# Layer 3 of a four-layer graph network: the new state turned by VectorE and transfers instead of TensorE

## The chip, the cores and the metric

The kernel runs on one core of one Trainium2 chip. The metric is the device time of a run in microseconds (us). The engines of a core, each with its own instruction queue that is worked off in order, are TensorE (matmuls; the profile calls it PE, and its loads of the stationary operand PEld), VectorE (DVE), ScalarE (ACT), GpSimd (POOL) and SyncE (SP), which here only issues transfers. SBUF is the working memory of 128 partitions, PSUM takes what TensorE writes, in 8 banks of 128 x 512 floats, and device memory holds inputs and outputs.

## The reference

128 graphs of 64 nodes with 256 features go through four layers, each of the form `x = layernorm(x + layer(x, adj))`, all in float32. Layers 0 to 2 are graph convolutions and are not touched here. Layer 3 is a gated graph network, five rounds with one set of gate weights:

```
A = (adj != 0)
h = x
for l in range(5):
    m   = h @ weight[l]
    agg = A^T @ m                      # for each graph
    gi, gh = agg @ w_ih.T + b_ih, h @ w_hh.T + b_hh
    r = sigmoid(gi_r + gh_r);  z = sigmoid(gi_z + gh_z)
    n = tanh(gi_n + r * gh_n)
    h = (1 - z) * n + z * h
out = layernorm(x + h * mask)
```

So each round needs the state `h` in two layouts. The gate products contract over features and take `h` with features in the partitions. The aggregation over neighbours contracts over nodes and takes `h` with nodes in the partitions. The gates produce the new state with features in the partitions.

## The kernel before

Two graphs make a pair of 128 nodes, and eight graphs (four pairs) make a chunk, so there are 16 chunks. A chunk's state with nodes in the partitions is a tile of 128 x 4 pairs x 256 features (`xt`, and from the second round on `h`); with features in the partitions it is 128 x 2 halves x 512 nodes (`hT`, and when new `hn`). `weight[l]` and `w_ih` are folded into one matrix `V[l]`, so that the aggregation works on `h` itself: `messages` calls `gather`, whose matmuls have the state as stationary operand (loaded into the array) and the 0/1 adjacency `A01` as moving operand, and ScalarE copies the result to `agg`.

The gate products are done by a scheme of seven products for a 2 x 2 block matrix: GpSimd forms sums of the operand (`sums`, tiles `Th` of the state and `Ta` of `agg`), and `rz(i)` (reset and update gate, four products each) and `n(i)` (candidate, two products each) are the seven products, i from 1 to 7, in an order that fits the accumulation in PSUM. VectorE and ScalarE bring the parts together. `n(7)`, `n(4)` and `n(3)` end the round: `reset` forms the candidate's argument, `update` does the tanh and the new state, first for the feature half j=1 (in `n(4)`), then for j=0 (in `n(3)`).

The loop over s (lines 985 to 1031) runs through 80 steps of one chunk and one round each; two chunks alternate. Step s does the products of chunk x and, laid in between, the rest of the work of the chunk w of the step before: `w.n(4)` and `w.n(3)` after the first products of x, then `w.turn(1)` and `w.turn(0)`, four TensorE transposes each, through PSUM and a ScalarE copy into `h` (in the last round VectorE adds it to `xt` from PSUM), and at last `w.close()`, which gathers for w's next round. `filler` lays in the work of layers 1 and 2 for the two chunks to come (`mid`), in pieces.

TensorE's instruction order is the program's own, as written. On the other engines a scheduler orders the instructions when the program is built; `high_priority` brings one forward. Tiles of one name share a fixed number of buffers (`bufs`), and a tile waits until the buffer's readers are done. PSUM banks of the gate products come from a pool of five (`pg`), all others of layer 3 from one of three (`pt`).

The lines that matter: L208 the gather's matmuls, L212 its copies, L757 the gate products, L774 copies of partial products, L798 transposes on TensorE, L941 the copy into `h`, L946 the last round's add, L737 to L739 the sums on GpSimd, L853 to L862 reset and update, L964 the stores of the output, L189 and L197 the loads of adjacency and of `x` for the chunks to come.

Of the kernel before, what the change touches and what calls it, by code (L numbers as in the profile page):

```python
# [9 lines left out]
F32 = mybir.dt.float32  # L10
AF = mybir.ActivationFunctionType
ALU = mybir.AluOpType
# [3 lines left out]
B, N, D, HID, L = 128, 64, 256, 512, 5  # L16
# [10 lines left out]
NCH = B // CB  # L27
NP = CB // 2
# [40 lines left out]
def gnn_stack(  # L69
# [33 lines left out]
    dram = ctx.enter_context(tc.tile_pool(name="dram", bufs=1, space=bass.MemoryType.DRAM))  # L103
# [10 lines left out]
    powers, evictions, relus, tanhs = [], [], [], []  # L114
# [52 lines left out]
    ov = out.rearrange("(c p two) n d -> c (two n) p d", p=NP, two=2)  # L167
# [24 lines left out]
    def load_x(c):  # L192
# [6 lines left out]
                )  # L199
        xts[c] = xt  # L200

    def gather(src, m, name, pool=keep, tag="ag", bufs=1):

        a = pool.tile([128, 2, NP * 128], F32, tag=tag, name=name, bufs=bufs)
        for k in range(2):
            p = psum("pa")
            for q in range(NP):
                nc.tensor.matmul(  # L208
                    p[:, q * 128 : (q + 1) * 128], src[:, q, k * 128 : (k + 1) * 128], m[:, q, :], start=True, stop=True
                )  # L210
            with tc.high_priority():
                nc.scalar.copy(a[:, k, :], p)  # L212
        return a
# [4 lines left out]
    def mid(c):  # L218
# [28 lines left out]
        poly = keep.tile([128, NP, 128], F32, tag="poly", name="poly3", bufs=2)  # L247
# [6 lines left out]
        AT1 = keep.tile([128, NP, 128], F32, name="AT1", bufs=1)  # L254
        p = psum("pT1").rearrange("p (q n) -> p q n", q=NP)
# [9 lines left out]
        xt = xts.pop(c)  # L265
        p = psum("pp").rearrange("p (q n) -> p q n", q=NP)
        for q in range(NP):
            nc.tensor.matmul(p[:, q, :], An[:, q, :], poly[:, q, :], start=True, stop=True)
        poly = keep.tile([128, NP, 128], F32, tag="poly", name="poly1", bufs=2)
        with tc.high_priority():  # L270
            nc.vector.scalar_tensor_tensor(poly, dg, cw[:, 1:2], p, op0=ALU.mult, op1=ALU.add)
        ag = gather(xt, AT1, "ag1")
        nc.vector.tensor_add(xt, xt, l1bs[:, None, :].to_broadcast([128, NP, D]))
        p = psum("pp").rearrange("p (q n) -> p q n", q=NP)
        for q in range(NP):
            nc.tensor.matmul(p[:, q, :], An[:, q, :], poly[:, q, :], start=True, stop=True)  # L276
        poly = keep.tile([128, NP, 128], F32, tag="poly", name="poly0", bufs=2)
# [19 lines left out]
        yield  # L297


        ag = gather(xt, poly, "ag2")  # L300
        yield
        for u in range(NP // 2):
            p = psum("pd").rearrange("p (q d) -> p q d", q=2)
# [484 lines left out]
    class Chunk:  # L788
# [11 lines left out]

        def state_of_layer2(self, k):
            if k:
                self.hT = work.tile([128, 2, NP * 128], F32, tag="hT", name="hT", bufs=4)
            p = self.transpose(lambda q, k: self.xt[:, q, k * 128 : (k + 1) * 128], k, "pT3")
            nc.scalar.copy(self.hT[:, k, :], p)
            if not k:
                self.th = sums(self.hT, "h")

        def messages(self, h=None):
            self.agg = gather(self.xt if h is None else h, self.A01, "agg", work, "agg", 2)  # L810
            self.ta = sums(self.agg, "a")

        def rz(self, i):
# [19 lines left out]
        def n(self, i):  # L833
            if i == 1:
                self.NI = keep.tile([128, 2, 2, NP * 128], F32, tag="NI", name="NI", bufs=2)
                self.gn = Gates(
                    self.NI, [[(V[self.l], 2, self.agg, self.ta)], [(WHH, 2, self.hT, self.th)]], "n"
                )
            self.gn.product(i)
            I, n, r = self.NI[:, 0], self.NI[:, 1], self.RZ[:, 0]  # L840
            if i == 7:
                self.reset(1, slice(H, 2 * H), I[:, 1, H:], n[:, 1, H:])
            elif i == 4:
                self.reset(1, slice(0, H), self.gn.a[:, 0, :], self.gn.a[:, 1, :])
                self.hn = work.tile([128, 2, NP * 128], F32, tag="hT", name="hn", bufs=4)
                self.update(1)
            elif i == 3:
                self.reset(0, slice(0, 2 * H), I[:, 0, :], n[:, 0, :])
                self.update(0)

        def reset(self, j, f, i, h):
            n, r = self.NI[:, 1], self.RZ[:, 0]
# [75 lines left out]

        def turn(self, k):

            last = self.l == L - 1
            if k:
                self.hT = self.hn
                if not last:
                    self.h = work.tile([128, NP, D], F32, name="h", bufs=1)
            p = self.transpose(lambda q, k: self.hT[:, k, q * 128 : (q + 1) * 128], k, "pT4")
            pv = p.rearrange("p (q f) -> p q f", q=NP)
            f = slice(k * 128, (k + 1) * 128)
            if not last:
                with tc.high_priority():  # L940
                    nc.scalar.copy(self.h[:, :, f], pv)  # L941
                if not k:
                    self.th = sums(self.hT, "h")
            else:
                for q in range(NP):
                    nc.vector.scalar_tensor_tensor(  # L946
                        self.xt[:, q, f], pv[:, q, :], mask[:, self.c * NP + q : self.c * NP + q + 1], self.xt[:, q, f],
                        op0=ALU.mult, op1=ALU.add,
                    )

        def close(self, norm=None):
            if self.l < L - 1:
                self.messages(self.h)
            else:
                if norm:
                    mv, rs, _ = norm
                    nb = small.tile([128, NP], F32, name="nb")
                    nc.vector.scalar_tensor_tensor(nb, mv[:, :, 0], -1.0, rs, op0=ALU.mult, op1=ALU.mult)
                    with tc.issue_after(tanhs[-1].ins):
                        norm_apply(self.xt, mv, rs, nb, "a")  # L960
                else:
                    layernorm(self.xt, "a")
                for h in range(2):
                    nc.sync.dma_start(ov[self.c][:, 2 * h : 2 * h + 2], self.xt[:, 2 * h : 2 * h + 2])  # L964
            self.l += 1

# [18 lines left out]
    for s in range(NCH * L):  # L985
        u, t = s // (2 * L) * 2, s % (2 * L)
        if t == 0:
            for _ in filler:
                pass
            if u + 2 < NCH:  # L990
                for c in (u + 2, u + 3):
                    load_adj(c)
                    load_x(c)
                filler = both(mid(u + 2), mid(u + 3))
        if s == NCH * L - 1:
            break
        x, w = rows[s % 2], before
        nxt = None
        x.rz(1)
        if w:  # L1000
            w.n(4)
        x.rz(2)
        if w:
            w.n(3)
        x.rz(6)
        next(filler, None)
        x.rz(5)
        x.rz(7)
        x.n(1)
        if w:  # L1010
            w.turn(1)
            if w.l == L - 1 and w.c + 2 < NCH:
                nxt = Chunk(w.c + 2)
                nxt.state_of_layer2(1)
        x.rz(4)
        if w:
            w.turn(0)
            if nxt:
                nxt.state_of_layer2(0)
        x.n(6)  # L1020
        x.rz(3)
        if w:
            w.close()
            if nxt:
                nxt.messages()
                rows[(s + 1) % 2] = nxt
        x.n(2)
        x.n(5)
        next(filler, None)
        x.n(7)  # L1030
        before = x

    x, w = rows[1], before
# [4 lines left out]
    w.n(4)  # L1038
    x.rz(2)
    w.n(3)  # L1040
    x.hn = work.tile([128, 2, NP * 128], F32, tag="hT", name="hn", bufs=4)
    x.NI = keep.tile([128, 2, 2, NP * 128], F32, tag="NI", name="NI", bufs=2)
    for i in (6, 5, 7):
        x.rz(i)
# [74 lines left out]
```

## Time and profile before

| | |
|---|---|
| median of 3 runs (lowest to highest) | 2191.71 us (2191.57 to 2192.38) |
| span of the profiled execution | 2190.0 us |
| instructions in it | 30124 |
| VectorE busy | 1357.1 us |
| ScalarE busy | 1003.3 us |
| GpSimd busy | 573.1 us |
| moved by transfers | 51.12 MB |

The profiled execution has only its span; it lies 1.7 us below the median of the runs. A group in the profile is read as: line, engine, operation, tile written <- tiles read, shapes, xcount | busy us, mean ns of one | us that the engine sat idle before it, and what ended that. An fp32 matmul counts as two instructions there, a transpose as one. The busy time of an engine is the time in which at least one instruction of its own was under way; TensorE's instructions overlap one another, so the step from one start to the next says more than a duration. The chain that ended last is followed back from the last instruction, at each step to what released it.

### The profile page before, as it was taken

The page shows a single profiled execution, that of the slowest core. Times are in us where ns is not written, and L with a number is a line of the kernel's source. Part 1 is how long each engine was busy: PE and PEld are TensorE (multiplying, and loading weights), DVE is VectorE, ACT ScalarE, POOL GpSimd, SP SyncE. Part 2 cuts the span into 40 slices and gives each one's busy share as a digit, 9 for nine tenths or more (in the row PEclk, how much of TensorE's full clock was granted, in tenths as well). Part 3 has the DMA queues.
Part 4 walks back from the last instruction along what each step waited for, and adds up shares of the span by engine and source line. Part 5 has one row for each costly group of instructions (what it writes and reads, how often), then busy time and mean ns, then how long its engine had stood idle before and what let it go on. Part 6 is the DMA issues. An engine that isn't in the chain of part 4 may idle for free.

```text
span 2190.0 us, 30124 instructions
## 1 busy us (share of the span) xinstructions
PE 2175.2 (99%) x11538; PEld 1908.2 (87%) x11538; DVE 1357.1 (62%) x3033; ACT 1003.3 (46%) x1846; POOL 573.1 (26%) x622
## 2 busy tenths in 40 slices
PE   9999999999999999999999999999999999999998
PEld 6777888898988889888889898889898898888887
DVE  3345666566766676666766666657656666566556
ACT  3333334544544554444444454445444544455454
POOL 3211131232332222222322232232222222232222
PEclk9999999999999999999999999999999999999999
DMA  6532110000100010000000010001000000000000
GB/s 166 180 120 67 48 38 3 1 3 1 42 1 3 1 39 4 3 1 20 22 3 1 1 42 1 3 1 42 1 1 1 20 10 1 1 10 11 1 1 20
DMA packets 54236, 51.12 MB, mean 23 GB/s; under 512 B 20942, under 2 KB 49100, under 8 KB 54092
## 3 DMA queue, kind: packets, MB, share of 16 engines
q1 hardware_dynamic: 49412, 43.95, 6.6%
q0 software_dynamic: 1968, 4.83, 0.8%
q8 instruction: 91, 1.49, 0.3%
q10 hardware_dynamic: 2712, 0.42, 0.1%
q14 instruction: 53, 0.43, 0.1%
HBM read 32.40 MB, written 16.78 MB: 22 GB/s over the span
## 4 chain that ended last, share of the span: by engine, by line
PE 97%; DVE 2%; POOL 0%; issue 0%; DMA 0%; ACT 0%; SPq 0%; POOLq 0%; DVEq 0%; ACTq 0%
PE parz L757 25%; PE pan L757 12%; PE pdrz L757 12%; PE pa L208 9%; PE pbrz L757 6%; PE pdn L757 6%; PE ps L458 4%; PE ph L442 4%; PE pT L798 4%; PE pbn L757 3%; PE pd L286 3%; PE pd L307 3%; PE pa L426 1%; PE po L480 1%; PE pf L578 1%; PE pp L276 1%
## 5 line engine op out<-in xcount | busy, mean ns | idle before, releaser
L774 ACT COPY c<-parz 128x512 f32<-128x512 f32 x240 | 140.6, 586 | 320.4 <-PE parz L757 319.8
L757 PE MATMUL parz<-Th,WHH 128*128 128x256 f32 x960 | 285.9, 379 | 0.2 <-ACT c L774 0.2
L757 PE MATMUL parz<-Ta,V 128*128 128x256 f32 x960 | 285.8, 379 | 0.0
L737 POOL TENSOR_TENSOR Th<-hn 128x512 f32<-128x512 f32 x64 | 81.4, 1272 | 725.2 <-DVE hn L862 602.8
L774 ACT COPY c<-pan 128x512 f32<-128x512 f32 x237 | 138.9, 586 | 149.7 <-PE pan L757 149.7
L859 ACT ACTIVATE NI<-NI,bih 128x512 f32<-128x512 f32 x158 | 113.9, 721 | 201.6 <-DVE NI L854 201.5
L757 PEld LDWEIGHTS parz<-Ta,V 128*128 128x128 f32 x960 | 182.5, 190 | 24.7
L757 PEld LDWEIGHTS parz<-Th,WHH 128*128 128x128 f32 x960 | 176.3, 190 | 21.2 <-ACT c L774 0.7
L831 ACT ACTIVATE RZ<-RZ,brz 128x512 f32<-128x512 f32 x158 | 114.7, 726 | 136.6 <-DVE RZ L786 136.6
L786 DVE TENSOR_TENSOR RZ<-pdrz,c 128x512 f32<-128x512 f32 x80 | 55.0, 688 | 191.7 <-PE pdrz L757 191.7
L737 POOL TENSOR_TENSOR Ta<-agg 128x512 f32<-128x512 f32 x80 | 101.9, 1274 | 266.1 <-ACT agg L212 266.1
L137 POOL TENSOR_TENSOR rs<-ve,mhalf 128x4 f32<-128x4 f32 (+2 forms) x65 | 67.2, 1035 | 286.1 <-DVE ve L135 222.9
L757 PE MATMUL pan<-Ta,V 128*128 128x256 f32 x474 | 141.3, 380 | 0.0
L757 PE MATMUL pan<-Th,WHH 128*128 128x256 f32 x474 | 141.1, 379 | 0.0
L780 DVE TENSOR_TENSOR NI<-pbn,c 128x512 f32<-128x512 f32 x79 | 54.6, 692 | 127.4 <-PE pbn L757 110.2
L208 PEld LDWEIGHTS pa<-A,h 128*128 128x128 f32 x1024 | 124.4, 192 | 3.3
L208 PE MATMUL pa<-A,h 128*128 128x128 f32 x1024 | 124.6, 275 | 0.0
L776 DVE TENSOR_TENSOR NI<-pdn,c 128x512 f32<-128x512 f32 x79 | 54.4, 689 | 113.0 <-ACT c L774 113.0
L860 DVE TENSOR_TENSOR RZ<-hn,NI 128x512 f32<-128x512 f32 x126 | 86.5, 686 | 48.5 <-ACT NI L859 48.5
L862 DVE TENSOR_TENSOR hn<-RZ,NI 128x512 f32<-128x512 f32 x158 | 108.4, 686 | 1.8
L861 DVE TENSOR_TENSOR RZ<-RZ 128x512 f32<-128x512 f32 x158 | 108.2, 685 | 1.8
L458 PE MATMUL ps<-W,hg 128*125 128x256 f32 (+5 forms) x464 | 103.6, 380 | 0.3 <-ACT v L313 0.3
(228 smaller groups left out, 5056.1 us busy)
## 6 DMA issues: line engine op xcount, KB each, us to landing
out_dram<-xt SPq DMA_DIRECT2D x30, 256.0 KB
W<-in_w_dram SPq DMA_DIRECT2D x10, 512.0 KB
xt<-xb SPq DMA_DIRECT2D x32, 156.0 KB
xo<-in_x_dram SPq DMA_DIRECT2D x9, 512.0 KB
xb<-xo SPq DMA_DIRECT2D x9, 512.0 KB
xt<-xa SPq DMA_DIRECT2D x32, 100.0 KB
xg<-in_x_dram SPq DMA_DIRECT2D x25, 125.0 KB
xa<-xg SPq DMA_DIRECT2D x25, 125.0 KB
```

What stands on the lines that cost most here:

```text
L208: nc.tensor.matmul(p[:, q * 128 : (q + 1) * 128], src[:, q, k * 128 : (k + 1) * 128], m[:, q, :], start=True, stop=True)
L442: nc.tensor.matmul(p, W1[:, u.g, k, e * 128 : (e + 1) * 128], ag0[:, k, : u.cols], start=k == 0, stop=k == 1)
L458: nc.tensor.matmul(p[: u.rows[t], t - v, :], hg[:, e, u.off[t] : u.off[t] + u.rows[t]], W2[:, u.g, e, :], start=e == 0, stop=e == 3,)
L737: nc.gpsimd.tensor_sub(t[:, 0:2, :], a[:, :, H:], a[:, 0, :].rearrange("p (s n) -> p s n", s=2))
L757: nc.tensor.matmul(bank[:, g, :], w[:, q, i - 1, :], rhs, start=i in (1, 2, 5) and g == 0 and m == 0, stop=m == len(side) - 1, skip_group_ ...
L774: nc.scalar.copy(c, self.a)
L798: nc.tensor.transpose(p[:, q * 128 : (q + 1) * 128], src(q, k), ident)
L831: nc.scalar.activation(RZ[:, q, 0, :], RZ[:, q, 0, :], AF.Sigmoid, bias=b[0])
L859: nc.scalar.activation(n, n, AF.Tanh, bias=bih[:, 4 + j : 5 + j])
L860: e.tensor_sub(d, self.hT[:, j, f], n)
L861: e.tensor_mul(d, d, z)
L862: e.tensor_add(self.hn[:, j, f], d, n)
```

## The change

A chunk's new state is no longer transposed by TensorE. A new function `flip` follows each `update`: VectorE transposes the state half in blocks of 32 x 32 into a tile `flip`, in which the four pairs lie innermost; SyncE stores that to a buffer `hb` in device memory; and after the second half four transfers, one for each 32 partitions, bring both halves back as `h`, now 128 x 256 features x 4 pairs. The gather of rounds 1 to 4 takes its stationary operand from there, a column of features with a step of four floats. In the last round VectorE adds from `h` to `xt` in `close`. Only for chunk 14's last round does `turn` remain.

`w.n(4)` and `w.n(3)` move out of the following step into their own, to its end; `n(2)` comes earlier; `w.close()` with the gather now comes after `x.n(7)`, ahead of `x.n(4)` and `x.n(3)`. The state's sums for GpSimd follow directly on the update. `hT` and `hn` have three buffers instead of four.

```diff
         def messages(self):
+            src = halves(self.xt)
+            if self.l:
+                h = self.h
+                src = lambda q, k: h[:, k * 128 : (k + 1) * 128, q]
+            self.agg = gather(src, self.A01, "agg", work, "agg", 2)
...
             elif i == 4:
...
-                self.hn = work.tile([128, 2, NP * 128], F32, tag="hT", name="hn", bufs=4)
+                self.hn = work.tile([128, 2, NP * 128], F32, tag="hT", name="hn", bufs=3)
                 self.update(1)
+                self.flip(1)
             elif i == 3:
                 self.reset(0, slice(0, 2 * H), I[:, 0, :], n[:, 0, :])
                 self.update(0)
+                self.flip(0)
+                if self.l < L - 1:
+                    self.hT = self.hn
+                    self.th = sums(self.hT, "h")
+
+        def flip(self, j):
+
+            if self.c == NCH - 2 and self.l == L - 1:
+                return
+            if j:
+                self.hb = dram.tile([2, 128, NP * 128], F32, name="hb", bufs=2)
+            with tc.high_priority():
+                t = work.tile([128, NP, 32, NP], F32, name="flip", bufs=2)
+                nc.vector.transpose(
+                    t.rearrange("p r f q -> p q r f"), self.hn[:, j, :].rearrange("p (q r f) -> p q r f", q=NP, r=NP)
+                )
+                nc.sync.dma_start(self.hb[j], t.rearrange("p r f q -> p (r f q)"))
+                if not j:
+                    self.h = work.tile([128, D, NP], F32, name="h", bufs=1)
+                    hv = self.hb.rearrange("j (a i) (r c) -> r i (j a) c", i=32, r=NP)
+                    for r in range(NP):
+                        nc.sync.dma_start(
+                            self.h[32 * r : 32 * (r + 1)].rearrange("p (a f) q -> p a (f q)", f=32), hv[r]
+                        )
...
         x, w = rows[s % 2], before
         nxt = None
-        x.rz(1)
-        if w:
-            w.n(4)
-        x.rz(2)
-        if w:
-            w.n(3)
-        x.rz(6)
+        for i in (1, 2, 6):
+            x.rz(i)
         next(filler, None)
         x.rz(5)
         x.rz(7)
         x.n(1)
-        if w:
-            w.turn(1)
-            if w.l == L - 1 and w.c + 2 < NCH:
-                nxt = Chunk(w.c + 2)
-                nxt.state_of_layer2(1)
+        x.n(2)
+        if w and w.l == L - 1 and w.c + 2 < NCH:
+            nxt = Chunk(w.c + 2)
+            nxt.state_of_layer2(1)
         x.rz(4)
-        if w:
-            w.turn(0)
-            if nxt:
-                nxt.state_of_layer2(0)
+        if nxt:
+            nxt.state_of_layer2(0)
         x.n(6)
         x.rz(3)
+        x.n(5)
+        next(filler, None)
+        x.n(7)
         if w:
             w.close()
             if nxt:
                 nxt.messages()
                 rows[(s + 1) % 2] = nxt
-        x.n(2)
-        x.n(5)
-        next(filler, None)
-        x.n(7)
+        x.n(4)
+        x.n(3)
         before = x
...
         def close(self, norm=None):
+            self.l += 1
+            if self.l < L:
+                self.messages()
+                return
...
+                for q in range(NP):
+                    m = self.c * NP + q
+                    y = self.xt[:, q, :]
+                    nc.vector.scalar_tensor_tensor(
+                        y, self.h[:, :, q], mask[:, m : m + 1], y, op0=ALU.mult, op1=ALU.add
+                    )
+                layernorm(self.xt, "a")
```

More of the change, by code (lines that the diff above doesn't have):

```diff
@@ L200, in load_x, with halves @@
         xts[c] = xt
+    def halves(x):
+        return lambda q, k: x[:, q, k * 128 : (k + 1) * 128]
     def gather(src, m, name, pool=keep, tag="ag", bufs=1):
@@ L207, in gather @@
             for q in range(NP):
-                nc.tensor.matmul(
-                    p[:, q * 128 : (q + 1) * 128], src[:, q, k * 128 : (k + 1) * 128], m[:, q, :], start=True, stop=True
-                )
+                nc.tensor.matmul(p[:, q * 128 : (q + 1) * 128], src(q, k), m[:, q, :], start=True, stop=True)
             with tc.high_priority():
@@ L271, in mid @@
             nc.vector.scalar_tensor_tensor(poly, dg, cw[:, 1:2], p, op0=ALU.mult, op1=ALU.add)
-        ag = gather(xt, AT1, "ag1")
+        ag = gather(halves(xt), AT1, "ag1")
         nc.vector.tensor_add(xt, xt, l1bs[:, None, :].to_broadcast([128, NP, D]))
@@ L297, in mid @@
         yield
-        ag = gather(xt, poly, "ag2")
+        ag = gather(halves(xt), poly, "ag2")
         yield
@@ L802, in state_of_layer2 @@
             if k:
-                self.hT = work.tile([128, 2, NP * 128], F32, tag="hT", name="hT", bufs=4)
+                self.hT = work.tile([128, 2, NP * 128], F32, tag="hT", name="hT", bufs=3)
             p = self.transpose(lambda q, k: self.xt[:, q, k * 128 : (k + 1) * 128], k, "pT3")
@@ L807, in state_of_layer2, with messages @@
                 self.th = sums(self.hT, "h")
-        def messages(self, h=None):
-            self.agg = gather(self.xt if h is None else h, self.A01, "agg", work, "agg", 2)
+        def messages(self):
+            src = halves(self.xt)
[3 more added lines that the diff above has]
+            self.agg = gather(src, self.A01, "agg", work, "agg", 2)
             self.ta = sums(self.agg, "a")
@@ L929, in turn @@
         def turn(self, k):
[L931 to L936, printed above, removed]
+            p = self.transpose(lambda q, k: self.hn[:, k, q * 128 : (q + 1) * 128], k, "pT4")
             pv = p.rearrange("p (q f) -> p q f", q=NP)
             f = slice(k * 128, (k + 1) * 128)
[L939 to L943, printed above, removed]
+            for q in range(NP):
+                m = self.c * NP + q
+                nc.vector.scalar_tensor_tensor(
+                    self.xt[:, q, f], pv[:, q, :], mask[:, m : m + 1], self.xt[:, q, f], op0=ALU.mult, op1=ALU.add
+                )
@@ L944, in turn, with close @@
+        def close(self, norm=None):
+            self.l += 1
+            if self.l < L:
+                self.messages()
+                return
+            if norm:
+                mv, rs, _ = norm
+                nb = small.tile([128, NP], F32, name="nb")
+                nc.vector.scalar_tensor_tensor(nb, mv[:, :, 0], -1.0, rs, op0=ALU.mult, op1=ALU.mult)
+                with tc.issue_after(tanhs[-1].ins):
+                    norm_apply(self.xt, mv, rs, nb, "a")
             else:
                 for q in range(NP):
+                    m = self.c * NP + q
+                    y = self.xt[:, q, :]
@@ L946, in turn @@
                     nc.vector.scalar_tensor_tensor(
-                        self.xt[:, q, f], pv[:, q, :], mask[:, self.c * NP + q : self.c * NP + q + 1], self.xt[:, q, f],
-                        op0=ALU.mult, op1=ALU.add,
-                    )
[L951 to L965, printed above, removed]
+                        y, self.h[:, :, q], mask[:, m : m + 1], y, op0=ALU.mult, op1=ALU.add
+                    )
@@ L970, in gnn_stack @@
+                layernorm(self.xt, "a")
+            for h in range(2):
+                nc.sync.dma_start(ov[self.c][:, 2 * h : 2 * h + 2], self.xt[:, 2 * h : 2 * h + 2])
     rows = []
@@ L1037, in gnn_stack @@
     x.rz(1)
-    w.n(4)
     x.rz(2)
-    w.n(3)
-    x.hn = work.tile([128, 2, NP * 128], F32, tag="hT", name="hn", bufs=4)
+    x.hn = work.tile([128, 2, NP * 128], F32, tag="hT", name="hn", bufs=3)
     x.NI = keep.tile([128, 2, 2, NP * 128], F32, tag="NI", name="NI", bufs=2)
```

## The prediction

> **What bounds the kernel now.** I read the engines' busy times, then the chain that ended last, whole and piece by piece in one stretch of layer 3.
>
> ```profile
> PE 2175.2 (99%) x11538; PEld 1908.2 (87%) x11538; DVE 1357.1 (62%) x3033; ACT 1003.3 (46%) x1846; POOL 573.1 (26%) x622
> PE 97%; DVE 2%; POOL 0%; issue 0%; DMA 0%; ACT 0%; SPq 0%; POOLq 0%; DVEq 0%; ACTq 0%
> ```
>
> TensorE is never without work, and 97% of the chain is its own. So the change is worth what it takes out of TensorE's row, less what it makes slower in that row and less any hole that it opens. A matmul's shown duration overlaps the next one's, so prices come from the chain in order of time (start, length, name, count):
>
> ```profile
> 644.12 0.86 PE pan L757 x4
> 644.99 0.44 PE pT L798 x4
> 645.42 1.73 PE parz L757 x8
> 647.15 0.44 PE pT L798 x4
> 647.59 0.86 PE pan L757 x4
> 648.46 1.73 PE pdrz L757 x8
> 650.18 1.78 PE pa L208 x16
> 651.97 0.87 PE pbn L757 x4
> ```
>
> An fp32 product appears as two passes: 0.216 us a pass of 256 columns, so 0.431 a product; the gather `pa` takes 1.78/16 = 0.111 us a pass of 128 columns; a turn `pT` takes 0.109. A step of one chunk and one layer is 42 products (18.1), 8 gather products (1.78) and 8 turns (0.87), 20.8 us in all.
>
> ```profile
> L208 PE MATMUL pa<-A,h 128*128 128x128 f32 x1024 | 124.6, 275 | 0.0
> L208 PEld LDWEIGHTS pa<-A,h 128*128 128x128 f32 x1024 | 124.4, 192 | 3.3
> L798 PE MATMUL pT<-ident,hn 128*128 128x128 f32 x632 | 94.8, 273 | 0.0
> L798 PEld LDWEIGHTS pT<-ident,hn 128*128 128x128 f32 x632 | 79.0, 141 | 15.9
> L941 ACT COPY h<-pT 128x512 f32<-128x512 f32 x128 | 75.3, 588 | 0.0
> ```
>
> The reader sees 632 turns of the state, and that every gather pass has its own load of 128 weights: there the load row is as busy as the matmul row. In the gather the state `h` is the loaded operand.
>
> **What the Trainium skill says.** "TensorE: Matmul & The Clock Gate", LDWEIGHTS: columns divided by 1.2 in ns, so 107 for 128; the gather's 111 ns a pass agrees, and says that it stands at the load's own rate. "Advanced Engine Details and Errata", Memory Cachelines: SBUF has lines of 16 bytes, and it takes at least two hits on a line to absorb the access latency; another line at every access is penalised. For VectorE the trace shows this, in layer 0's sums:
>
> ```profile
> L502 DVE TENSOR_TENSOR F<-F,z 128x384 f32<-128x384 f32 x4 | 2.2, 549 | 0.0
> L502 DVE TENSOR_TENSOR F<-F,z 128x126 f32<-128x126 f32 x8 | 2.0, 288 | 4.6 <-ACT z L484 4.6
> L502 DVE TENSOR_TENSOR F<-F,z 128x64 f32<-128x64 f32 x4 | 1.1, 271 | 3.9 <-ACT z L484 3.9
> L502 DVE TENSOR_TENSOR F<-F,z 128x6 f32<-128x6 f32 x8 | 0.9, 159 | 0.0
> ```
>
> `F` has 15 floats a graph. The 384 and 126 elements are in runs of six and three, and with the 6 they lie on one line: 1.03 ns an element. On it the 64 should take 219 ns; they are in runs of one, 60 bytes apart, and took 271: 52/64 = 0.81 ns more an element, 1.8 times the rate. "VectorE: DVE Perf Modes", The three transpose paths: blocks of 32x32 only, 311 ns for 128x128 in bf16; no run here shows one. "DMA: Bandwidth & Descriptors", Latency and other measured facts: some 2 us of fixed cost; the queue of SyncE agrees:
>
> ```profile
> 1027.78 1.36 SPq L964 DMA_DIRECT2D out_dram<-xt  x2
> 1030.95 0.28 SPq L197 DMA_DIRECT2D xt<-xa  x1
> ```
>
> The load waits for the second store of 256 KB, issued at 1028.75: it landed after 2.2 us.
>
> **The change, part by part.**
>
> Turns. Of 632, the 8 of the chunk before the last remain. 624 x 0.109 = 68 us off the row that sets the end. Their 128 copies (75.3 us of ScalarE) and the last layer's adds from PSUM cost and give nothing directly: ScalarE is 46% busy and no step of the chain.
>
> Gather. `h` becomes 256 features by 4 pairs, so the 128 weights of a pass lie 16 bytes apart, each on a line of its own; before they were adjacent. Layers 1 to 4 of 16 chunks do it: 64 gathers, 1024 passes. The trace has no such load, so I bound it. Below: nothing (the load may not be limited by the line); a gain has no reason. Above: VectorE's 0.81 ns, or half the rate, gives 128 x 0.81 = 104 ns or 107 ns more a pass; and if what is fixed is VectorE's 1.85 ns a line, 237 ns a pass, 126 more. I take half the rate: 1.66 us a gather, and 64 of them 106 us (129 at most). The loads cannot hide, since the matmul beside each needs only 0.107. The whole turns at 68/1024 = 66 ns a pass: above it the change loses, below it wins.
>
> Transposes. 156 on VectorE, read in order, written 16 bytes apart. Four of the skill's price is 1.24 us, an ordinary 128x512 takes 0.69, and 512 x 0.81 on top of that gives 1.1: I take 1.1, ends 0.7 and 1.6. That is 172 us (109 to 250) onto VectorE's 62%. The cover is TensorE's step; uncovered, it counts only through the lateness of `h`.
>
> Transfers. 156 stores of 256 KB and 312 loads of 128 KB on SyncE's queue, 82 MB more than the 51 now, or some 45 GB/s over layer 3; the early slices show 180. Bandwidth is no matter, latency is. Take the end of `n(3)` as 0. `n(4)` ended at -0.9. VectorE then has the two resets of `n(4)` (0.9), an add (0.6), the long reset (1.3) with the tanh under it, both updates (3.6), one 0.6 of the next chunk, and the two transposes (2.2), at the back-to-back spacing of its rows (0.6 for a shown 0.69): last transpose done near 8.7. Store 2.2 to 3.0 (3.0 is the slowest seen in layer 0's stores). Four issues of 0.4 put the last load 1.2 later, and it lands 2.0 to 3.1 after that: `h` is there at 14.3 to 16.2. The gather now stands behind 38 products, at 16.4. So it is covered with 0.2 to 2.1 us to spare; steps with work of layers 0 to 2 laid in give TensorE up to 7 us more, but the step that holds the adjacency's preparation adds some 6 us to VectorE and only 0.4 to TensorE. I count 0.5 us in 14 such steps: 7 us, ends 0 and 40. The only buffer of `h` is free: the gather that read it ended some 15 us before. Two waits now have the state's transfers queued behind them on SyncE: a store of the output that waits for ScalarE's norm, with loads of `xt` that wait for that store's landing (2.2 us, as above), and a load of adjacency that waits for a VectorE read. Who waits in the end is the gather. At 2.2 us in each of 14 chunks that is 31 us, inside the ends. In the last layer VectorE itself waits for `h` (56 adds of 128x256), with the add for `n(7)` and the resets queued behind it, whose reader is the next chunk's bank 5 us later: if `h` is in time as above, nothing.
>
> Order. `n(4)` and `n(3)` move into their own step, behind the gather. Behind it come `n(4)` and `n(3)` (4 products), `rz(1)` and `rz(2)` of the other chunk (8) and one of `rz(6)` before GpSimd's sums `Ta` are needed: 13 products, 5.6 us. In the trace it is 3.0 us from the gather's end (1003.59) to the end of L738 on GpSimd (1006.56). The evicted `agg` is needed 5 products (2.1 us) after the gather; an eviction takes 0.58. A PSUM bank is asked for again at the soonest some 2 us after its reader (`rz(4)`'s sigmoids, then `n(5)`). `hT` with 3 buffers holds the three states alive at a time. All at nothing: the products named are the cover, and without it each us late is a us of hole per step, 80 in all.
>
> Sum against the span of 2190.0: -68 + 106 + 7 = 2235; the median of the runs stands 1.7 above the span, so 2236.7, say 2236.
>
> **Rivals.**
>
> *Loads at full rate.* If TensorE's port has line rate to spare, the gather stays at 0.111. For it: the skill's TensorE page puts weights at 1.2 a ns but columns at 2.4, and no TensorE row here shows a penalty. Against: 0.81 ns in the L502 row. Then 2190 - 68 + 7 + 1.7 = 2131. This one ends on the other side, from 66 ns a pass down.
>
> *The state comes late.* If transposes take 1.6 (+1.0), or loads in 512-byte pieces land in 5 us instead of 3, `h` is 2 us past the gather in nearly every step: 64 x 2 = 128 us of holes, as waits of `pa` for a transfer. 2357 with the slow loads, 2259 without. Against: the sum above leaves time even at the long ends of both transfers.
>
> *No difference.* A partial penalty near 66 ns with the holes at nothing: 2188 to 2196. Only coincidence speaks for it.
>
> **How the numbers follow.** Half rate, `h` in time: 0.49, own range 2208 to 2265 (a price of 85 to 129 us, holes of 0 to 40). Full rate, in time: 0.31, 2122 to 2170. A penalty of some 20 to 50 ns a pass: 0.04, 2145 to 2180. Late state: 0.13. Nothing: 0.03. The predicted time is the first case's, 2236. From 2124 to 2265 the range holds most of the first two and a little of the third: 8 in 10. A measurement tells 0.2%, 4.4 us, from no change. Faster: the second and third case, 0.35; slower: the first and the late state, 0.62; within, 0.03.
>
> **What would show it.** `pT` at 136 passes in all (8 of the state, 128 of layer 2). `pa` from `h`: starts 0.21 us apart against 0.11, and a gather of 3.4 us in the chain; gathers of layer 0, from `xt`, still 1.78. Transposes near 1.1 us. TensorE idle before `pa` under 10 us, by transfers. Wrong if the gather stays at 1.78 (then near 2131), or if TensorE's busy share falls under 97% with transfers named in the waits.

## The result and the profile after

The changed kernel takes 2286.1 us (median of 4 runs, 2284.8 to 2287.8) against 2191.6 before on the same chip: the ratio is 1.043 with an interval of 1.0416 to 1.0446. It is slower by 94 us. The forecast had the sign, but at 2236 it was 50 us short, and its range ended at 2265. The profiled execution has a span of 2284.0 us, against 2190.0.

From the first and the fourth part of the page after, the busy times and the shares of the chain:

```profile
PE 2237.1 (98%) x10914; PEld 1965.4 (86%) x10914; DVE 1575.7 (69%) x3133; ACT 953.2 (42%) x1718; POOL 611.1 (27%) x622
PE 80%; DVE 14%; DMA 2%; ACT 1%; issue 1%; POOL 1%; SPq 0%; ACTq 0%; POOLq 0%; DVEq 0%
```

624 instructions are gone from TensorE, and yet it is busy for 62 us longer. Outside its busy time lie 46.9 us of the span, where before there were 14.8. The chain, once 97% TensorE's own, goes through VectorE for 14%. So two things grew, the work of TensorE and its holes, and the next two views take them in turn. The groups with shapes kept apart (busy us, mean ns | idle before):

```profile
L212 PE MATMUL pa<-A,h 128*128 128x128 f32 x1024 | 244.3, 393 | 9.2 <-DMA h<-hb 9.2
L870 DVE STREAM_TRANSPOSE flip<-hn 128x512 f32<-128x512 f32 x156 | 178.5, 1144 | 2.0
L212 PE MATMUL pa<-A,xt 128*128 128x128 f32 x256 | 31.2, 275 | 0.0
```

The gather from `h` went from a mean of 275 ns a pass to 393; the gather from `xt`, whose weights are adjacent, kept its 275. From start to start the 1024 passes take 233.7 us against 114.2 before, so 119.5 us more, 117 ns a pass on average; inside a gather a pass follows the last after 0.233 us, where it was 0.112. In the chain, in one plain step:

```profile
1015.86 3.62 PE pa L212 x16
```

1.78 us has become 3.62. And the waits of TensorE (us in all, times, longest), where before only two turns at the end stood out in layer 3:

```profile
PE parz L759 <- ACT c L776: 11.9, 16, 1.1
PE pp L278 <- DVE poly L273: 10.1, 13, 1.1
PE pa L212 <- DMA h<-hb: 9.2, 7, 4.1
```

(`parz` and the like are the PSUM tiles of the gate products; `pp` is a small product in the work of the first layers for the chunks to come.) Of these three the forecast had the third. By the product that stands before each in the trace, the 16 waits of the first kind are seven of `rz(7)` for the copy of `rz(6)`, 7.9 us, eight of `rz(4)` for the copy of `rz(7)`, 3.8 us, and one at the end. One of the seven, on ScalarE and then on TensorE (start, length, name; in brackets the idle time before it and its releaser):

```profile
1068.81 0.72 ACT L890 ACTIVATE NI<-NI,bih 128x512 f32<-128x512 f32 x1 [2.55 <-DVE NI L885]
1069.77 1.58 ACT L149 ACTIVATE xt<-xt,nb,rs 128x256 f32<-128x256 f32 x3 [0.24 <-DVE nb L141]
1071.26 0.56 ACT L776 COPY c<-parz 128x512 f32<-128x512 f32 x1
```

```profile
1070.17 0.59 PE L759 MATMUL pdrz<-Ta,V 128*128 128x256 f32 x2
1071.88 0.70 PE L759 MATMUL parz<-Th,WHH 128*128 128x256 f32 x2 [1.11 <-ACT c L776]
```

The copy of `rz(6)` could start when that product ended, at about 1068.8. ScalarE works in order: ahead of the copy stand a tanh, which waited 2.55 us for VectorE, and three pieces of the last layer's norm, which waited for VectorE too. `rz(7)` writes the bank that the copy reads, so TensorE stood for 1.11 us. The same two lines give the price of a hole. From 1070.17 to 1071.88 are 1.71 us, where two passes take 0.43: 0.17 more than the 1.11 shown. The two passes behind the hole take another 0.1 longer (0.70 for 0.59). Over the 17 holes between gate products in this trace the medians are 0.16 and 0.11. So a hole costs what it shows and some 0.27 us on top, called refilling below.

One of the second kind:

```profile
598.97 1.95 PE L212 MATMUL pa<-AT,xt 128*128 128x128 f32 x16
601.96 1.16 PE L278 MATMUL pp<-poly,An 128*128 128x128 f32 x8 [1.04 <-DVE poly L273]
```

`poly`'s operand, the first `pp`, was ready at 599.1, as the gather `ag1` began. VectorE wrote `poly` only from 601.17 to 601.90, behind the last layer's adds and norm statistics of another chunk and a piece of an update.

### The profile page after: what moved, and what is told of

It reads as the page before. It is cut to its first block, busy times and chain, and to the rows that moved or that the text cites. A ratio compares the mean times of both kernels' runs of the same rounds, so it can differ in the third digit from the quotient of the medians.

```text
span 2284.0 us, 29716 instructions
## 1 busy us (share of the span) xinstructions
PE 2237.1 (98%) x10914; PEld 1965.4 (86%) x10914; DVE 1575.7 (69%) x3133; ACT 953.2 (42%) x1718; POOL 611.1 (27%) x622
## 4 chain that ended last, share of the span: by engine, by line
PE 80%; DVE 14%; DMA 2%; ACT 1%; issue 1%; POOL 1%; SPq 0%; ACTq 0%; POOLq 0%; DVEq 0%
PE parz L759 19%; PE pa L212 12%; PE pdrz L759 10%; PE pan L759 10%; PE pdn L759 5%; PE pbrz L759 4%; PE ps L460 4%; PE ph L444 4%; PE pbn L759 2%; PE pd L309 2%; PE pd L288 2%; DVE xt L986 1%; DVE flip L870 1%; DVE NI L884 1%; DMA h<-hb 1%
## 5 line engine op out<-in xcount | busy, mean ns | idle before, releaser
L759 PE MATMUL parz<-Th,WHH 128*128 128x256 f32 x960 | 287.2, 381 | 11.9 <-ACT c L776 11.9
L212 PEld LDWEIGHTS pa<-A,h 128*128 128x128 f32 x1024 | 243.8, 328 | 13.6 <-issue 7.7
L212 PE MATMUL pa<-A,h 128*128 128x128 f32 x1024 | 244.3, 393 | 9.2 <-DMA h<-hb 9.2
L739 POOL TENSOR_TENSOR Th<-hn 128x512 f32<-128x512 f32 x64 | 87.0, 1360 | 408.7 <-DVE hn L893 378.0
L870 DVE STREAM_TRANSPOSE flip<-hn 128x512 f32<-128x512 f32 x156 | 178.5, 1144 | 2.0
L214 ACT COPY agg<-pa 128x512 f32<-128x512 f32 x160 | 93.8, 586 | 168.6 <-PE pa L212 167.5
L837 ACT ACTIVATE RZ<-RZ,brz 128x512 f32<-128x512 f32 x158 | 105.4, 714 | 134.4 <-DVE RZ L788 134.4
L884 DVE SCALAR_TENSOR_TENSOR NI<-NI,bhh,RZ 128x256 f32<-128x256 f32 (+1 forms) x158 | 107.8, 682 | 3.8
```

The costliest lines, as they stand in the source:

```text
L212: nc.tensor.matmul(p[:, q * 128 : (q + 1) * 128], src(q, k), m[:, q, :], start=True, stop=True)
L759: nc.tensor.matmul(bank[:, g, :], w[:, q, i - 1, :], rhs, start=i in (1, 2, 5) and g == 0 and m == 0, stop=m == len(side) - 1, skip_group_ ...
L837: nc.scalar.activation(RZ[:, q, 0, :], RZ[:, q, 0, :], AF.Sigmoid, bias=b[0])
L870: nc.vector.transpose(t.rearrange("p r f q -> p q r f"), self.hn[:, j, :].rearrange("p (q r f) -> p q r f", q=NP, r=NP))
L884: nc.vector.scalar_tensor_tensor(n[:, j, f], h, bhh[:, 4 + j : 5 + j], r[:, j, f], op0=ALU.add, op1=ALU.mult)
```

## The experiments

Twelve kernels were run. Their TensorE rows are put together in the balance at the end of this section.

**1. Adjacent weights in the changed kernel.** Only the operand of the gather's loads is changed:

```diff
-                src = lambda q, k: h[:, k * 128 : (k + 1) * 128, q]
+                h = h.rearrange("p f q -> p (f q)")
+                src = lambda q, k: h[:, (2 * q + k) * 128 : (2 * q + k + 1) * 128]
```

> The changed kernel, but the gathers of rounds 1 to 4 load 128 adjacent floats of h instead of 128 floats four apart (so they gather other numbers of the same tile). Theory S, the step of 16 bytes makes the load slow: a gather falls from 3.6 us to 1.8, 64 of them are 119 us, so 2286 - 119 = 2167 us (2155 to 2180). Rival T, the loads are slow because transfers write SBUF beside them or because the tile was just landed: a gather stays above 3 us and the time near 2286.

2192.0 us, ratio 1.000 (0.9992 to 1.0009). The pass is back at 278 ns, so the step between the weights, and nothing else about `h`, makes the load slow. But of the 116.8 us by which the gathers got shorter only 94 came back, because the holes grew, as TensorE's waits in this run show:

```profile
PE parz L759 <- ACT c L776: 26.4, 34, 1.4
PE pp L278 <- DVE poly L273: 14.7, 13, 1.4
```

With the loads as fast as before, the 68 us of turns taken away are all eaten by holes. Of the 34 waits for a copy 18, with 14.5 us, are of `rz(6)` for the copy of `rz(1)`. The changed kernel has none of these, and its own 16 are all here again. The slow gather, it seems, had been hiding the 18: it gave ScalarE and VectorE 119.5/64 = 1.87 us more a step.

**2. The step alone, in the kernel before.** The copy from PSUM writes `h` with the four pairs innermost, and the gather reads it so; turns and order stay:

```diff
-                    nc.scalar.copy(self.h[:, :, f], pv)
+                    nc.scalar.copy(self.h[:, f, :].rearrange("p f q -> p q f"), pv)
```

> The kernel before, in which ScalarE's copy writes h as 256 features by 4 pairs, so that the gather loads with a step of four floats; no transfer, no change of order. Theory S: a pass of the gather goes from 112 to 232 ns, 2192 + 119 = 2311 us (2300 to 2320). Rival T: no transfers, so 2192. A slower copy on ScalarE is hidden in both (46% busy).

2309.5 us, 1.0538 (1.0522 to 1.0553): 118 us for the step alone, without a new hole. The gather among this run's groups:

```profile
L211 PE MATMUL pa<-A,h 128*128 128x128 f32 x1024 | 242.5, 390 | 0.0
```

The two runs give nearly the same price from both sides: start to start, 115 ns a pass put in here and 114 taken out in the first. The forecast's turning point was 66.

**3. Transposes that write adjacent numbers.**

```diff
-                t = work.tile([128, NP, 32, NP], F32, name="flip", bufs=2)
+                t = work.tile([128, NP, NP, 32], F32, name="flip", bufs=2)
-                    t.rearrange("p r f q -> p q r f"), self.hn[:, j, :].rearrange("p (q r f) -> p q r f", q=NP, r=NP)
+                    t.rearrange("p r q f -> p q r f"), self.hn[:, j, :].rearrange("p (q r f) -> p q r f", q=NP, r=NP)
```

> The changed kernel, but VectorE's transposes write adjacent floats (the pairs of h come out in another order, so the numbers are other ones). The transposes should fall from 1144 ns to about 690 (60 us of VectorE in all). Theory H, the holes before pp and before the gather come from VectorE being late: they shrink from 22 us to under 10, 2286 - 12 = 2274 us. Rival: those holes come from where the work of layers 1 and 2 stands in VectorE's order, and stay: 2284 or more.

2273.4 us, 1.0372 (1.0357 to 1.0388): 13 us less. First the transposes among its groups, then TensorE's waits:

```profile
L870 DVE STREAM_TRANSPOSE flip<-hn 128x512 f32<-128x512 f32 x156 | 110.2, 707 | 2.0
```

```profile
PE parz L759 <- ACT c L776: 9.6, 10, 1.1
PE pp L278 <- DVE poly L273: 8.0, 11, 1.1
PE pa L212 <- DMA h<-hb: 4.3, 2, 3.5
```

The 0.44 us that each transpose pays for its step is 68 us of VectorE's time, and TensorE feels 13 of them, in all three kinds of wait.

**4. Without the last layer's adds.** The 56 adds of L986, which the turned kernel makes from `h`, are left out.

```diff
-                    nc.vector.scalar_tensor_tensor(
-                        y, self.h[:, :, q], mask[:, m : m + 1], y, op0=ALU.mult, op1=ALU.add
-                    )
```

> The changed kernel without the 56 adds of h to xt in the last round (left out of the computation for 14 of the 16 chunks). Theory A, these adds hold up VectorE and through it ScalarE's copy for rz(6): the 16 holes before parz (16 us) go, 2286 - 16 = 2270 us. Rival: the layernorm behind them (statistics, GpSimd's power, ScalarE's scaling) holds up ScalarE, and the holes stay: 2284.

2286.5 us, 1.0432 (1.0417 to 1.0448): no gain. `parz` waited 9.3 us instead of 11.9, `pp` 8.0 and `pa` 1.8, but `pan` waited 8.1 us for a copy, where it had waited 0.7. The seven waits of `rz(7)` are gone, so the adds had a part in them; `rz(4)` waits 13 times instead of eight. Taking 41 us of work from VectorE at these places moves the holes and doesn't close them.

**5. The new order alone.** The kernel before, with its turns on TensorE and its adjacent `h`, gets the changed kernel's order of products:

```diff
-        x.rz(1)
-        if w:
-            w.n(4)
-        x.rz(2)
-        if w:
-            w.n(3)
-        x.rz(6)
+        for i in (1, 2, 6):
+            x.rz(i)
...
+        x.n(4)
+        x.n(3)
```

> The kernel before with the changed order of products alone (n(4) and n(3) in their own step behind the gather, n(2) early), turns still on TensorE and adjacent loads. Theory O, the order itself makes holes, because only rz(2) (1.7 us) lies between rz(1) and rz(6) for ScalarE's copy, which stands behind a tanh: 10 to 25 us more, 2202 to 2217. Rival V, the holes need the transposes and adds that load VectorE: 2192, within 4 us.

2221.1 us, 1.0134 (1.0119 to 1.0149): the order alone costs 29 us. The forecast had it at nothing. One of its 15 waits of `parz`, 14 of which are of this kind, on TensorE and then on ScalarE:

```profile
857.25 0.59 PE L757 MATMUL pbrz<-agg,V 128*128 128x256 f32 x2
858.84 0.67 PE L757 MATMUL parz<-Th,WHH 128*128 128x256 f32 x2 [0.99 <-ACT c L774]
```

```profile
857.50 0.72 ACT L859 ACTIVATE NI<-NI,bih 128x512 f32<-128x512 f32 x1 [4.21 <-DVE NI L854]
858.13 0.56 ACT L774 COPY c<-parz 128x512 f32<-128x512 f32 x1
```

`rz(1)` ended near 855.9, and its copy could have started there. It starts at 858.13, behind the tanh, which waited for VectorE's reset L854, whose own engine was in a norm of another chunk. On GpSimd and VectorE at that time:

```profile
854.10 1.26 POOL L737 TENSOR_TENSOR Ta<-agg 128x512 f32<-128x512 f32 x1
854.16 2.15 DVE L152 TENSOR_SCALAR xt<-xt,mv,rs 128x256 f32<-128x256 f32 x2 [0.90 <-POOL rs L137]
857.05 0.41 DVE L854 TENSOR_TENSOR NI<-pan,NI 128x256 f32<-128x256 f32 x1
```

In the old order `n(4)`, `rz(2)` and `n(3)` lay between `rz(1)` and `rz(6)`, 3.45 us of cover; in the new one `rz(2)` alone, 1.73. And the resets and the tanh of `n(4)` now fall into just that stretch.

The two norm pieces took 2.15 us beside GpSimd's sum of `agg`, where in the kernel before none took over 0.42. This holds for the whole run: with the same instructions VectorE is busy for 1442.0 us instead of 1357.1, and GpSimd for 613.5 instead of 573.1. Of VectorE's 1142 instructions on two operands of 128x512, those with no GpSimd instruction beside them take 0.68 us on average in both kernels, 0.69 at most; over 0.9 us took 14 before and 86 here, every one beside a GpSimd instruction. So the new order also lays GpSimd's sums beside VectorE's work, and both get longer there. How much of the 29 us comes from that was not tried alone.

**6. The same order with the copy first.** The update of the state is traced behind the other chunk's `rz(1)`, and its tanh is issued after that product's copy:

```diff
+        def finish(self, other):
+            self.hn = work.tile([128, 2, NP * 128], F32, tag="hT", name="hn", bufs=4)
+            with tc.issue_after(other.g.copied.ins):
+                self.update(1)
+            self.update(0)
...
         x.rz(1)
+        if w:
+            w.finish(x)
```

> The kernel before in the new order alone, turns by TensorE and adjacent loads (2221.1 us), with the tanh after the copy of rz(1). Theory C: of the 29.3 us that the order cost, 14.0 us in 15 waits of parz for ScalarE's copy and 0.2 us of refilling each go: 2204 us. Rival E: the copy is not the cause but whatever fills VectorE behind the gather; the wait moves to pp and pdn: 2215 us or more.

2204.1 us, 1.0056 (1.0041 to 1.0071), as expected. In the timeline of ScalarE the copy now stands first, in the same step:

```profile
851.57 0.59 ACT L774 COPY c<-parz 128x512 f32<-128x512 f32 x1 [2.92 <-PE parz L757]
852.85 0.72 ACT L862 ACTIVATE NI<-NI,bih 128x512 f32<-128x512 f32 x1 [0.69 <-DVE NI L857]
```

The wait of `parz` falls from 14.0 us to one of 0.2. So 17 of the order's 29 us were the update's place ahead of the copy. The edit moves the update's VectorE work along with its tanh; but only the waits of `parz` went, while those of `pp` and `pdn` for VectorE stayed (6.5 us in the fifth run, 6.3 here), which points to the tanh in ScalarE's queue. Most of the other 12 us are these waits with 13 refillings. VectorE is still busy for 1440.9 us.

**7. A step of two.** `h` as two halves, each with two pairs innermost; the transposes write, and the transfers carry, pairs of floats:

```diff
-                src = lambda q, k: h[:, k * 128 : (k + 1) * 128, q]
+                src = lambda q, k: h[:, q // 2, k * 128 : (k + 1) * 128, q % 2]
-                    self.h = work.tile([128, D, NP], F32, name="h", bufs=1)
+                    self.h = work.tile([128, 2, D, 2], F32, name="h", bufs=1)
```

> The changed kernel with h as 2 pairs of pairs by 256 features by 2, so that a load has a step of two floats, two of them on each line of 16 bytes; the transposes write with the same step, and pieces of a transfer fall from 512 to 256 bytes. Theory S in its form of lines (two hits on a line are enough): a gather near 1.8 us and transposes near 700 ns, so the time of the kernel with adjacent loads less the gain of shorter transposes, 2192 - 12 = 2180 us (2172 to 2192). If any step costs: gathers near 2.7 us or more, over 2235. If the smaller pieces come late: holes before the gather of more than 20 us, over 2195.

2197.3 us, 1.0026 (1.0015 to 1.0037). The gather passes stand 0.118 us apart (120.3 us for all, against 114.2 and 233.7), with a mean of 281 ns, and the transposes take 712 ns. Two floats a line restore nearly the whole rate, on both engines. The 2180 that was expected is missed by the holes: `parz` waits 38.0 us in 26 times.

**8. A step of two, and the copy first.** The last kernel with the edit of the sixth.

> The same with a step of two, and the tanh of the new state (with what follows it) is issued behind ScalarE's copy for rz(1) of the other chunk instead of ahead of it. Theory O, the copy stands behind a tanh that waits for VectorE: the holes before parz (26 us with adjacent loads) fall under 8, so 15 to 20 us faster than the kernel with a step of two alone, 2155 to 2168. Rival: the copy is late for another reason (the rows of VectorE), no more than 5 us between the two; or the later tanh makes h late, and the holes move to the gather.

2183.3 us, 0.9964 (0.9953 to 0.9975): 14 us under the seventh, and 8 under the kernel before, the only one of the twelve that is more than 0.2% faster than it. TensorE's waits in it:

```profile
PE pp L278 <- DVE poly L273: 20.8, 12, 2.9
PE parz L759 <- ACT c L776: 4.4, 15, 0.3
```

Some 34 us of waiting for the copy have gone, and 13 have come back at `pp`.

**9. And `pp` apart.** In the stage of the next chunk's first layers, for all chunks but the first two, a `yield` goes between the gather `ag1` and the second `pp`:

```diff
         ag = gather(halves(xt), AT1, "ag1")
         nc.vector.tensor_add(xt, xt, l1bs[:, None, :].to_broadcast([128, NP, D]))
+        if apart:
+            yield
         p = psum("pp").rearrange("p (q n) -> p q n", q=NP)
```

> The last kernel (steps of two, copy ahead of the tanh; 2183.3 us) with the second group of products pp of the next chunk's first layers put at its own place in TensorE's order, one filler later, and not right behind the gather ag1. Theory P: TensorE stands 20.8 us in 12 waits of pp for VectorE's poly only because pp follows a gather of 1.8 us after VectorE got its last operand; apart, the wait is gone: about 20.8 + 12 x 0.2 less, 2160 us. Rival Q: VectorE is behind its work at these places anyway and the next product that needs it waits instead: 2175 us or more.

2190.4 us, 0.9992 (0.9985 to 0.9999): the theory falls. `pp` no longer waits for `poly`, but `parz` waits 17.5 us for copies again, and `pdn`, `pdrz` and `pa` some 4 each. As in the fourth run, a hole shut at one place opens at the next one that needs VectorE or stands behind it.

**10 and 11. The two edits in the changed kernel itself**, with its step of four.

> The changed kernel (steps of four) with the update and the turns of a chunk traced behind the other chunk's rz(1), and the tanh issued after ScalarE's copy of rz(1). Theory C: the copy behind the tanh is what rz(6) waited for, 11.9 us in 16 waits and some 0.2 us of refilling each: 2286 - 15 = 2271 us. Rival D: the turns come later by the wait for the copy, and h comes later at the gather: that wait, 9.2 us in 7 now, takes 10 us or more in addition: 2280 us or more.

> The changed kernel with both: the tanh after the copy of rz(1), and the second group of pp one filler later. Theory: both kinds of holes go, 11.9 + 10.1 us of standing and 29 refillings of 0.2 us: 2286 - 28 = 2258 us, which leaves the slow loads alone: 2191.7 - 68 + 120 + some 14. Rival: holes only move to the next wait (h, or a product that needs VectorE): 2275 us or more.

2303.8 us (1.0511, 1.0496 to 1.0527) and 2303.4 (1.0509, 1.0494 to 1.0525): they are 18 and 17 us slower than the changed kernel, and both theories fall. In the tenth, seven of the `parz` waits are 2.06 us where they were 1.1, as at 581.11:

```profile
581.11 0.70 PE L759 MATMUL parz<-Th,WHH 128*128 128x256 f32 x2 [2.06 <-ACT c L776]
```

They are those of `rz(7)` for the copy of `rz(6)`, of the kind shown above at 1071. There the tanh does not stand in front of the copy of `rz(1)`. With the edit it started 4.1 us after that copy instead of 3.1, with the norm's pieces behind it, and all of them still in front of the copy of `rz(6)`. The expectation had taken all waits of `parz` in the changed kernel for the one of the fifth run. In the eleventh the waits of `pp` are gone, as expected, but those of `pa` for `h` grew from 9.2 to 17.0 us, in 13; why there and not in the tenth, where they are 7.5, was not tried.

**12. The old places with turns through memory.** The kernel of the seventh run with `n(4)` and `n(3)` back between the next step's products; the gather stays behind `n(7)`.

> The kernel with steps of two (2197.3 us) with n(4) and n(3) back at the places of before, between the products of the other chunk's next step; the gather stays behind n(7). It tells what the order of the change buys: the copy for rz(1) has n(4), rz(2) and n(3) ahead of rz(6) again, and h has less time. From the end of n(3) to the last load of h took some 15 us in a step of the changed kernel (648.5 to 663.5 us), 14 with the faster transposes; between n(3) and the gather lie five products of 1.72 and five of 0.86 us, 12.9 us, and the fillers. Theory L: h is late by 1 to 2 us in the steps without a filler, and by nothing in the others: 2190 - 68 + 6 + 30 to 80 = 2160 to 2210 us, with the waits of pa in place of those of parz. Rival N: with VectorE less behind, h comes in time: 2130 to 2150 us, and no new order was needed.

2236.7 us (2231.4 to 2244.3), 1.021 (1.0183 to 1.0236), slower than either case expected. TensorE's waits:

```profile
PE pa L212 <- DMA h<-hb: 71.8, 38, 3.8
PE parz L759 <- ACT c L776: 0.2, 1, 0.2
```

This is the other half of the fifth run. The old places leave no wait for the copy, and `h` is late in 38 of 64 gathers, by 1.9 us on average. These 72 us are within the 80 that were expected; what goes beyond is the refilling and ten stretches at half clock, some 17 us. The new order is what buys the time for the transfers, and 29 us is its price where the turns are left on TensorE.

**The balance.** All terms are us of TensorE's row against the kernel before. Idle is the span less the busy time, less 14.8; holes are those over 60 ns in the trace beyond the nine of the kernel before, at 0.27 us each. After some holes the trace shows TensorE at half clock for 3.4 us, which costs 1.7 us of work; in run 8 one such stretch is twice as long. Passes at half clock are in two columns: in run 1 they are the gather's 2.7 us.

| kernel | turns | gather | idle | refilling | half clock | sum | span measured |
|---|---|---|---|---|---|---|---|
| the changed kernel | -68 | +119.5 | +32.1 | 37: +10.0 | 2: +3.4 | +97 | +94.0 |
| 1, adjacent loads | -68 | +2.7 | +53.1 | 56: +15.1 | 2: +3.4 | +6 | +2.3 |
| 3, adjacent flips | -68 | +118.5 | +23.3 | 25: +6.8 | 1: +1.7 | +82 | +80.5 |
| 5, order only | 0 | 0 | +20.4 | 29: +7.8 | 0 | +28 | +29.3 |
| 6, order, copy first | 0 | 0 | +7.3 | 14: +3.8 | 0 | +11 | +12.1 |
| 7, step of two | -68 | +6.1 | +47.9 | 46: +12.4 | 3: +5.1 | +3 | +5.5 |
| 8, and copy first | -68 | +6.7 | +35.4 | 44: +11.9 | 3: +6.8 | -7 | -8.5 |

The sums meet the spans within 4 us.

## Why the prediction was wrong

**Turns: right.** The terms of the balance close with 68 us in every kernel without them, and `pT` has the 136 passes named.

**Gather: the right mechanism, mis-sized.** Half rate gave 106 us; it measured 119.5. (The 106 are 1024 times 104 ns, VectorE's price; half of the gather's own rate of 112 ns is 115 us.) VectorE's 1.85 ns a line, which the forecast quoted for its upper end (237 ns a pass), was the better estimate: 0.233 us over 128 weights is 1.82 ns each. This is 13 of the 50 us.

**Transposes and transfers: right.** 1144 ns against 1.1 us, and for the reason given: the third run takes the step away and has 707, so the step costs 0.85 ns an element against 0.81. The wait for `h`, 9.2 us in 7 times against 7 us in 14, is under the 10 us named, but its sum is in part luck: a single wait near the end is 4.1 of it. (The times named for `h` add to 14.1 to 16.0 us, not 14.3 to 16.2.) In the plain step of the forecast's kind `h` was in time.

**Order: this step failed.** "All at nothing" checked the sums of GpSimd, the copy of `agg`, the PSUM banks and the buffers of `hT`. It didn't ask what happens to ScalarE's copies of the products: they stand in one queue with tanhs and norms that wait for VectorE, and the next product but one needs the bank. The fifth run puts the order at 29 us, and the sixth shows 17 of them to be the copy of `rz(1)`. In the changed kernel none of the 16 waits is this one: the slow gather, as the first run suggests, hides it, and the 16 are the copies of `rz(6)` and `rz(7)`, behind other work in the same queue. What the order costs there was not run alone. Nor did the step ask what GpSimd's sums do to VectorE's work beside them: the VectorE instructions that both kernels share take 52 us more in the changed one. The sentence that ScalarE is "46% busy and no step of the chain" read an average for a queue that works in order; in the changed kernel it is 42% busy, and it holds TensorE up 16 times.

**The cover of VectorE: it failed too.** "Uncovered, it counts only through the lateness of `h`" was wrong: the added VectorE work is felt at `poly` and through the tanh as well, and the third run gives 13 us for the step of its writes. The idle time grew by 32 us and not by 7, and 37 holes paid 10 us of refilling, for which the sum had no term. With the two half-clock stretches, 3 us, these are 38 of the 50 us. I can't split them by engine further than the runs do: runs 4, 9 and 11 show that the waits replace one another.

**The range.** Its own bounds, 129 us of gather and 40 of holes, add to 2293, but the range stopped at 2265, as if both could not come high together. They did: 119.5, and 46 of idle, refilling and half clock.

**The rivals.** Loads at full rate ended at 2131 in the forecast. The first run makes that case true by force, and the time was 2192: even there the forecast would have been 61 us short, by the same step, with a gain foretold where there was none. The late state is what the twelfth run shows for the old places, at 38 of 64 gathers.

## What to carry to other kernels

When an edit moves work between two steps of a software pipeline, list for every engine what then stands in its queue ahead of each copy out of PSUM, and what that waits for; a mean busy share of 42% says nothing on it. Ask too which work will now run side by side on VectorE and GpSimd. Holes on the bound engine are not closed one by one: price a change by taking its suspected cause alone, then its order alone, as runs 2 and 5 do here. If data must lie with a step in SBUF, keep two floats of each line in use together.

## What the runs showed of the hardware

- A load of 128 fp32 weights and its pass follow the last after 112 ns from adjacent floats, 118 at a step of two floats and 233 at a step of four. VectorE's 128x512 fp32 transpose takes 707 ns writing adjacent floats, 712 at pairs of them and 1144 at a step of four. In the Trainium skill the page "SBUF — State Buffer", Specifications (TRN2), asks for two hits on a line of 16 bytes for full bandwidth. The step of two, which gives two, agrees on both engines; for one hit the page names a penalty without its size, and here that is 2.1 times the time on TensorE and 1.6 on VectorE.
- VectorE's 128x512 fp32 instructions on two operands take 0.68 us with no GpSimd instruction beside them, in the kernel before and in run 5. The 86 that took over 0.9 us in run 5, and the 82 in the changed kernel, all ran beside one.
- Apart from the one in which every kernel ends, the half-clock stretches of one run begin whole multiples of 3.413 us apart. In runs 7 and 9 each of the eight stretches followed a piece of this grid with 2.02 to 2.23 us of holes in it, and no piece with 1.98 or less was followed by one. Of the two in the changed kernel, the one at 2094.8 us followed a piece with 2.13 us of holes; the one at 1115.2 a piece with only 0.59 us, but with 12 slow passes of the gather. Run 2 has the slow passes without new holes and no such stretch, so they alone don't bring it. In the Trainium skill the page "TensorE: Matmul & The Clock Gate", What's actually happening, has the clock halved after an idle window of about 3.4 us; here a window with 2.02 us of holes was enough.
